# A decoder layer in float32: all gate and up weights prepared beside the attentions, three pairs of blocks by two levels, one look at the kept sums

## The chip, the cores and the metric

The kernel runs on one core of a Trainium2 chip. The metric is the device time of one execution in microseconds (us). The kernel before took 2239.64, 2241.54 and 2240.38 us in three runs; their median is 2240.38 us.

## The reference

x has 16 batches of 128 rows and 1024 columns, all in float32. Three sublayers follow one another, each on a layer norm (LN) and each added to x:

```python
x = x + attn(LN(x))           # one head of 256: softmax(q k^T / 16) v, then Wo
x = x + xattn(LN(x), ctx)     # "linear attention", 8 heads of 64
x = x + ffn(LN(x))            # h = silu(g) * u; h @ Wd^T
```

In the cross attention, queries come from LN(x) and keys and values from a second input. Queries pass through a softmax over the 64 entries of a head, keys through a softmax over the 1024 places of the sequence. A head's context is the product of its keys and values, queries are multiplied with it and projected, and each column of the result is divided by its length.

In the feed-forward part g and u are products of 1024 with 2752 columns (gate and up) and the way back is one of 2752 with 1024 (down). The weights are given as 4-bit numbers, two to an integer. Each group of 64 along a row has a scale and a zero point, and a weight is (number - zero) * scale.

## The kernel before, in words

**Strassen.** The feed-forward products use Strassen's scheme: a product of 2x2 blocks with seven multiplications in place of eight. The 2752 columns of gate and up form eleven blocks of 256 (`BLOCKS`, L42); the last, `RB` = 10, is smaller. `one_block` (L1178) uses one level: 14 products (seven of gate, seven of up), each of four matmuls with 512 columns. `two_levels` (L1360) takes a pair of blocks and uses Strassen twice: seven outer products, each with seven inner ones of four matmuls with 256 columns, 196 in all. Its operands are sums made in time: `ti` (right, by VectorE, `Operands.inner_right`, L1305) and `li` (left, by GpSimd, `inner_left`, L1338). In the trace a float32 matmul shows as two instructions.

**Passes.** The feed-forward part does eight batches (8 to 15) in pass 0 and the other eight in pass 1, and each pass goes over all blocks. `PAIRS` (L1068) lists the pairs that pass 0 does by two levels: only pair 3 (blocks 6 and 7). So its order is blocks 0 to 5, pair 3, blocks 8 and 9, and the last block (`last_block`, L1207). Pass 1 does all five pairs by two levels, then the last block. The down projection follows.

**Preparation of the weights.** `prepare` (L205) is a generator; each `next` is a step of work for VectorE. For each matrix of a block it takes two halves, loads them (`load_raw`, L172, on SyncE's queue, SP), splits the 4-bit numbers (two TENSOR_SCALARs into `pa`) and applies zero point and scale (two TENSOR_TENSORs). A third step makes four sums (`comb`, into `pc`). The seven Strassen combinations are stored to device memory (`wprep`). Gate and up of blocks 0 to 4 (`EARLY` = 5, L286) are prepared within the self attention, with stores on GpSimd's queue (L309). All the rest (gate and up of blocks 5 to 10, and down of all blocks, alternating) is prepared beside the blocks of pass 0, step by step from `beside` (L1567) and from the `between` of `two_levels`. `attention_done` (L1036) starts that.

**The cross attention.** The batch loop (L941 to L966) handles batch k and prepares batch k+1. Each batch has eight ticks: four `key_unit`s (L711) of the next batch and four `query_unit`s (L784) of its own, alternating. What comes later hangs in a list by hand: `later(n, fn)` (L616) runs fn n ticks on. A key unit makes keys (`kq`), their exponentials (`ek`, ScalarE, L727), their sum over the batch (`ksum`, VectorE) and the product with the second input (`kx`). After the fourth, `mix` (L755, two ticks later) forms the context and multiplies it into one matrix `m_sb`. A query unit makes queries and their exponentials (`qe`, ScalarE, L795). One tick later `weigh` (L802) sums each head's exponentials (`qden`), takes the reciprocal (`qrec`) and lets GpSimd multiply (`qe` times `qrec`, L806). Another tick later `turn` (L811) transposes the result on VectorE (`kt`). It is stored and read back in another order as `qs` by SP's queue. `project_out` (L848) multiplies `qs` with `m_sb`. The norms follow (L871 to L878: a square, then Ln and Exp on ScalarE). At the start, loads stand on SP in this order: the cross attention's four weight matrices and two small ones (L641 to L646), the second input for two batches (`cx` and `cxt`, L925), and `wo_again`, the output weights of the self attention, whose last batches are projected here (L926 to L937). `mix_weights` (L674) multiplies value and output weights per head. It runs before the first batch.

**Checks on the sums.** The kernel guards against overflow. `note` (L656) adds every batch's sums of exponentials and their reciprocals into two running totals on GpSimd. `raise_flag` (L662) compares the totals with a limit and counts the partitions that are within it, by one small matmul. If not all are, `kernel` (L1831) runs a slower form of the layer. `preload_act_table_set` (L672) loads one table of functions for ScalarE that holds both Ln and Exp.

**Weight loads.** `load_weights` (L1077) loads the prepared tiles in the order `to_load`, `AHEAD` = 4 of them (L1056) before the first block: the first on GpSimd's queue, the others on SP (L1561). The rows of x for pass 1 are loaded by `block_loads` (L551), one step after every third product of blocks 8 and 9.

Of the kernel before, what the change touches and what calls it, by code (L numbers as in the profile page):

```python
# [18 lines left out]
P = 128  # L19
# [47 lines left out]
def decoder_layer(  # L67
# [95 lines left out]
    def prep_pools(stack, name, c, ahead):  # L163
        for key, bufs in (("a", 3), ("c", c), ("raw", ahead + 1), ("sz", ahead + 1)):
            pools[key] = stack.enter_context(
                tc.tile_pool(name=f"{name}_{key}", bufs=bufs, side="right", reuse_waits="tile")
            )
# [4 lines left out]
    def load_raw(blk, mat, s):  # L172
# [3 lines left out]
        if mat == "d":  # L176
            raw, sz = raw[:w], pools["sz"].tile([P, 2, 512], F32, name="szd")[:w]
            nc.sync.dma_start(raw, dq[ds(start // 2, w), ts(s, 512)])
            for g in range(w // 32):
                row = dsz[start // GROUP + g, ts(s, 1024)].rearrange("(t f) -> t f", t=2)  # L180
                nc.sync.dma_start(sz[ts(g, 32)], row.partition_broadcast(32))
# [13 lines left out]
        for m, off, w in parts:  # L195
            q, szs = matrices[m]
            nc.sync.dma_start(raw[:, :, ds(at, w)], q[:, :, ds(off, w)])
            nc.sync.dma_start(
# [6 lines left out]
    def prepare(jobs, ahead, queue, vector=nc.vector):  # L205
# [3 lines left out]
        loads = deque(load_raw(*u) for u in units[:ahead])  # L209
# [6 lines left out]
        for k, (blk, mat, s) in enumerate(units):  # L216
# [6 lines left out]
            if k + ahead < len(units):  # L223
                loads.append(load_raw(*units[k + ahead]))
# [61 lines left out]
    EARLY = 5  # L286

    def give_half(b, h, oT, wo_d, psum, tensor=nc.tensor, vector=nc.vector):
# [19 lines left out]
    prep_pools(first, "q", 4, 1)  # L308
    early = prepare(  # L309
        [(blk, mat) for blk in range(EARLY) for mat in "gu"], 1, nc.gpsimd, InOrder(tc, nc.vector)  # L310
    )
    give_pool = ExitStack()
    ag = give_pool.enter_context(tc.tile_pool(name="a_g", bufs=1, reuse_waits="tile"))
    with (
# [166 lines left out]
        for t in range(NT):  # L481
# [38 lines left out]
            else:  # L520

                for i in range(1, BPT):
                    give((t - 1) * BPT + i - 1, oT)
                    value(i, xnT, v)
                atT = turn_weights(at)
# [76 lines left out]
    bcx = unit_pool("b_cx", 2)  # L602
    bw = unit_pool("b_w", 1)
    b0 = unit_pool("b_0", 2)
    bek = unit_pool("b_ek", 3)
    bas = unit_pool("b_as", 1)
    b3 = unit_pool("b_3", 3)
    bkt = side_pool("b_kt", 3)
# [3 lines left out]
    bqs = side_pool("b_qs", 5)  # L612
    b1 = side_pool("b_1", 1)
    b2 = side_pool("b_2", 2)
    bps = side_pool("b_ps", 3, space=PSUM)

# [15 lines left out]
    if True:  # L632
        wq_sb = bw.tile([P, HIDDEN], F32, name="wq_sb")
# [7 lines left out]
        sync.dma_start(wk_sb, xwk)  # L641
        sync.dma_start(wq_sb, xwq)
        sync.dma_start(wv_sb, xwv.rearrange("(r p) s -> p r s", p=P))
        sync.dma_start(xwo_sb, xwo.rearrange("(r p) o -> p r o", p=P))
        sync.dma_start(xbo_sb, xbo)
        sync.dma_start(gs_sb, xg)  # L646
        vector.tensor_scalar(gs_sb, gs_sb, math.sqrt(S), None, ALU.mult)
        vector.memset(ones, 1.0)
        if plain:

            totals = [bs.tile([P, 2 * HEADS], F32, name=f"total{n}") for n in range(2)]
            for t in totals:
                nc.gpsimd.memset(t, 0.0)

        def note(*both):
            if plain:  # L656
                for t, v in zip(totals, both):
                    t = t[:, : v.shape[1]]
                    nc.gpsimd.tensor_tensor(t, t, v, ALU.add)

        def raise_flag():

            within = [small.tile([P, 1], F32, name=f"within{n}") for n in range(2)]
            for w, t in zip(within, totals):
                vector.tensor_reduce(w, t, AX.X, ALU.add)
                vector.tensor_scalar(w, w, LIMIT, None, ALU.is_le)
            vector.tensor_tensor(within[0], within[0], within[1], ALU.mult)
            ps = bps.tile([P, 1], F32, name="mm")
            tensor.matmul(ps, ones, within[0], start=True, stop=True)
            vector.tensor_copy(flag, ps[0:1])  # L670

        tc.keep_in_program_order(nc.scalar.preload_act_table_set("natural_log_exp_and_others"))  # L672
# [16 lines left out]

        def load_ctx(b):  # L690
            c = bcx.tile([P, C], F32, name="cx")
            sync.dma_start(c, cx[b])
            ct = bct.tile([P, NB, S], F32, name="cxt")
            sync.dma_start(ct, cxt[b])
            return c, ct
# [15 lines left out]
        def key_unit(ctx, p, st):  # L711
# [17 lines left out]
            def use():  # L729
# [16 lines left out]
                if p == 3:  # L746
# [4 lines left out]
                    later(2, lambda: mix(st))  # L751
# [3 lines left out]
        def mix(st):  # L755
# [7 lines left out]
            ksum, krec = (small.tile([P, 4], F32, name=name) for name in ("ksum", "krec"))  # L763
            vector.tensor_copy(ksum, ks)
            vector.reciprocal(krec, ksum)
            note(ksum, krec)
# [17 lines left out]
        def query_unit(xn, pair, qs, wait):  # L784
# [3 lines left out]
            for i in range(2):  # L788
                tensor.matmul(
                    ps[:, i, :], xn[:, ts(2 * pair + i, P)], wq_sb, start=True, stop=True  # L790
# [11 lines left out]
            def weigh():  # L802
                den, rec = (small.tile([P, 2 * HEADS], F32, name=n) for n in ("qden", "qrec"))
# [3 lines left out]
                note(den, rec)  # L807
# [114 lines left out]


        batches = [p + i for p in PASSES for i in range(HB)]
        ctxs = {b: load_ctx(b) for b in batches[:2]}  # L925
        wo_again = []  # L926
        for d in range(2):
            wo_again.append(bqs.tile([P, C], F32, name="wo_again", tag="qs"))
            sync.dma_start(wo_again[d], wo[ts(d, P)])
        mix_weights()  # L930
# [7 lines left out]
        keys = {b: {} for b in batches}  # L938
# [3 lines left out]
        for k, b in enumerate(batches):  # L942
# [13 lines left out]
            if len(ahead) == 2:  # L956
                later(2, lambda n=ahead[1]: ctxs.update({n: load_ctx(n)}))
# [3 lines left out]
            for oc in range(4):  # L961
# [3 lines left out]
                query_unit(xns[b], oc, qs, 4 if len(ahead) == 2 else 3)  # L965
# [60 lines left out]
    with ExitStack() as gs:  # L1026
# [9 lines left out]
        def attention_done():  # L1036

            nonlocal rest
            if plain:
                raise_flag()  # L1040
            sides.close()
            prep_pools(second, "f", 4, 2)
            jobs = []
            down = deque((blk, "d") for blk in range(len(BLOCKS)))
# [856 lines left out]
```

## Time and profile before

| | |
|---|---|
| median of three runs | 2240.38 us |
| the profiled execution | 2241.3 us |
| its span in the trace | 2239.5 us |
| instructions | 24114 |
| DMA | 425.23 MB, mean 190 GB/s |
| self attention | 0 to 250 us |
| cross attention | 250 to 757 us, a batch every 31.2 us |
| gate and up, pass 0 | 757 to 1297.5 us |
| of it pair 3 by two levels | 1074.6 to 1163.6 us |
| gate and up, pass 1 | 1297.5 to 1760 us |
| down projection | 1760 to 2239.5 us |

All times are from the profile of one execution. Its engines are TensorE (PE: matmuls; PEld: its weight loads), VectorE (DVE), ScalarE (ACT), GpSimd (POOL) and SyncE (SP, which issues DMAs). A row of the windows gives a stretch of time, its length, and the busy time and number of instructions of PE, PEld, DVE, ACT and POOL. After these come the granted clock of PE, the share of time in which the DMA engines were busy, and GB/s. A row of the waits gives engine, tile and line of the waiting instruction, what it waited for, the total in us, the number of waits and the longest. A row of the timeline gives start, duration, engine, line, operation, and output from input; a wait stands in brackets. L63 is the line of a helper (`InOrder`, L55) that keeps instructions in the order of the program, so one goes by the names of the tiles.

### The profile page before, as it was taken

Reading aid. Unit: us, or ns where it says so; the run is one execution under the profiler, and the core shown is the slowest. Engines: PE = TensorE matmul, PEld = TensorE weight load, DVE = VectorE, ACT = ScalarE, POOL = GpSimd, SP = SyncE. Lnnn points to the kernel's source line nnn. Section 1 sums busy time; section 2 is a strip of 40 time slices with the busy share of each in tenths; the row PEclk is TensorE's granted clock in tenths of the full one; section 3 lists DMA queues with packets and bytes.
Section 4 is the critical chain, followed back from the end, with each engine's and each line's share of the span. In section 5 each row is a group of like instructions: output and inputs, shape, how many; then the busy total and the mean of one; then the engine's idle time right before and its main releaser. Section 6 shows DMA issues by size and latency. Waiting matters only on the chain.

```text
span 2239.5 us, 24114 instructions
## 1 busy us (share of the span) xinstructions
PE 2204.4 (98%) x8330; PEld 1517.3 (68%) x8330; DVE 1482.2 (66%) x2055; ACT 468.9 (21%) x651; POOL 553.1 (25%) x543
## 2 busy tenths in 40 slices
PE   8999899999999999999999999999999999999998
PEld 7556555555555544444774488888887688888887
DVE  6997466667667657666796658787787645544462
ACT  2111135454554431111111112121121000000000
POOL 5452044444444400001320044444442000000000
PEclk9999999999999999999999999999999999999999
DMA  6435246666686768887649834454554964333731
GB/s 251 157 130 169 85 132 198 209 205 197 208 258 192 225 182 287 284 267 253 199 166 301 251 100 158 167 197 155 175 198 165 350 211 164 114 125 129 226 118 39
DMA packets 270835, 425.23 MB, mean 190 GB/s; under 512 B 28784, under 2 KB 130544, under 8 KB 270576
## 3 DMA queue, kind: packets, MB, share of 16 engines
q1 hardware_dynamic: 244624, 377.72, 52.5%
q0 software_dynamic: 8064, 27.27, 3.3%
q10 hardware_dynamic: 18016, 18.62, 2.7%
q8 instruction: 68, 1.11, 0.2%
q14 instruction: 63, 0.52, 0.1%
HBM read 265.62 MB, written 157.35 MB: 189 GB/s over the span
## 4 chain that ended last, share of the span: by engine, by line
PE 90%; DVE 6%; issue 2%; DMA 1%; POOL 1%; ACT 0%; SPq 0%; DVEq 0%; POOLq 0%; ACTq 0%
PE po L1780 21%; PE q L63 20%; PE p L63 18%; PE kq L63 9%; PE mm L63 8%; PE kx L63 5%; PE mm L396 4%; PE mm L411 2%; DVE pa L63 2%; PE p L1157 1%; PE mm L292 1%; PE tr L343 1%; DVE ti L63 1%; DMA wo_again<-in_wo 0%; POOL qe L806 0%
## 5 line engine op out<-in xcount | busy, mean ns | idle before, releaser
L63 PE MATMUL p<-b,w 128*128 128x512 f32 x560 | 248.2, 596 | 1.9 <-DVE sg L63 1.9
L63 PE MATMUL q<-ti,li 128*128 128x256 f32 x1008 | 232.2, 379 | 3.5 <-DVE ti L63 2.8
L63 POOL TENSOR_TENSOR li<-w 128x512 f32<-128x512 f32 x84 | 118.1, 1408 | 433.3 <-DMA w<-wu 244.8
L63 PEld LDWEIGHTS q<-ti,li 128*128 128x128 f32 x1008 | 191.0, 190 | 31.3 <-issue 2.8
L63 PEld LDWEIGHTS p<-b,w 128*128 128x128 f32 x560 | 106.9, 191 | 136.4 <-issue 128.8
L1780 PE MATMUL po<-wc,lc 128*128 128x256 f32 x840 | 183.4, 379 | 0.0
L63 PE MATMUL p<-T,w 128*128 128x512 f32 x400 | 177.2, 592 | 0.0
L1780 PEld LDWEIGHTS po<-wc,lc 128*128 128x128 f32 x840 | 159.6, 190 | 21.8
L63 ACT COPY k<-q 128x512 f32<-128x512 f32 x126 | 73.7, 585 | 399.2 <-PE q L63 399.2
L63 PEld LDWEIGHTS p<-T,w 128*128 128x128 f32 x400 | 76.0, 190 | 95.7 <-issue 95.2
L1780 PE MATMUL po<-wq,lq 128*128 128x256 f32 x560 | 126.7, 379 | 0.2 <-issue 0.2
L806 POOL TENSOR_TENSOR qe<-qe,qrec 128x1024 f32<-128x1024 f32 x64 | 122.0, 1906 | 11.5 <-DVE qrec L63 9.3
L63 PEld LDWEIGHTS mm<-qs,m_sb 128*128 128x128 f32 x512 | 97.3, 190 | 40.1 <-issue 26.8
L63 PE MATMUL kq<-wk_sb,cx 128*128 128x512 f32 x256 | 120.4, 592 | 2.5 <-DMA cx<-in_cx 2.5
L63 PE MATMUL kx<-ek,cxt 128*128 128x512 f32 x256 | 121.8, 598 | 0.0
L63 PE MATMUL mm<-qs,m_sb 128*128 128x256 f32 x512 | 120.8, 379 | 0.0
L63 PE MATMUL kq<-wq_sb,xn 128*128 128x512 f32 x256 | 120.3, 593 | 0.0
L1780 PEld LDWEIGHTS po<-wq,lq 128*128 128x128 f32 x560 | 106.0, 190 | 15.8 <-issue 0.8
L63 DVE TENSOR_TENSOR pa<-pa,sz 128x1024 f32<-128x1024 int32 x86 | 112.6, 1309 | 2.5
L396 PE MATMUL mm<-xnT,wqkv_sb 128*128 128x512 f32 (+1 forms) x320 | 112.9, 509 | 0.0
L63 DVE STREAM_TRANSPOSE kt<-qe 128x1024 f32<-128x1024 f32 x64 | 79.5, 1242 | 43.7 <-POOL qe L806 43.5
L727 ACT ACTIVATE ek<-kq 128x1024 f32<-128x1024 f32 x64 | 65.3, 1020 | 147.4 <-PE kq L63 147.4
(201 smaller groups left out, 3595.7 us busy)
## 6 DMA issues: line engine op xcount, KB each, us to landing
w<-wu SPq DMA_DIRECT2D x140, 256.0 KB, 3.6
lq<-h SPq DMA_DIRECT2D x140, 256.0 KB, 4.4
w<-wg SPq DMA_DIRECT2D x138, 256.0 KB, 2.8
kd<-kt SPq DMA_DIRECT2D x64, 512.0 KB, 2.9
qs<-kd SPq DMA_DIRECT2D x256, 128.0 KB, 3.2
h<-hc SPq DMA_DIRECT2D x80, 256.0 KB, 2.8
wq<-wd SPq DMA_DIRECT2D x70, 256.0 KB, 5.3
h<-h SPq DMA_DIRECT2D x60, 256.0 KB, 3.0
```

The costliest lines, as they stand in the source:

```text
L63: return lambda *args, **kw: self._tc.keep_in_program_order(fn(*args, **kw))
L292: tensor.matmul(ps, oT[:, d, ts(b % BPT, S)], wo_d[d][:, ts(h, 512)], start=(d == 0), stop=(d == 1),)
L343: nc.tensor.transpose(tr[:, j, :], xn[:, ts(4 * h + j, P)], ident)
L396: nc.tensor.matmul(ps[:, tokens], wqkv_sb[:, f, c, :], xnT[:, c, tokens], start=(c == 0), stop=(c == CC - 1),)
L411: nc.tensor.matmul(ps, xnT[:, c, ts(i, S)], wqkv_sb[:, 4:6, c, :], start=(c == 0), stop=(c == CC - 1),)
L727: nc.scalar.activation(ek, ps, AF.Exp)
L806: nc.gpsimd.tensor_tensor(qe, qe, rec.unsqueeze(2).to_broadcast(wide), ALU.mult)
L1157: tensor.matmul(ps, wt[:, j, :], T[q][:, :, j], start=(first == q and j == 0), stop=(q in (2, 3, 4) and j == JC - 1), skip_group_check=True,)
L1780: nc.tensor.matmul(bank[:, i, :], l[:, ts(i, S)], w,  start=(start and c == 0 and i % 2 == 0), stop=(stop and c == len(pairs) - 1), skip_g ...
```

## The change

1. A list `todo` holds all jobs of preparation: gate and up of blocks 0 to 9, the last block's two, then all of down. The self attention takes 11 of them (before: 10), with three more steps at its end. A second generator, `middle`, takes the other 11 of gate and up and runs within the cross attention. Batches 0, 2, 4, 6 and 8 take three steps, the other batches up to 12 take two. Its loads and stores stand on SP in the order of the program. Only down is left for the blocks.
2. `PAIRS` is [2, 3, 4]: pass 0 does blocks 0 to 3 by one level, blocks 4 to 9 by two, then the last block. The steps of preparation per pair fall from three to two, and those beside the blocks move.
3. The sums of exponentials are kept, each in its own columns of one tile `sums` (128 x 1088). `raise_flag` looks at their largest and smallest once, after the attention; the counting matmul comes two ticks later. `note` and the additions on POOL are gone.
4. `preload_act_table_set` is gone. The built program has 36 table loads where there were 9.
5. The first loads of the cross attention have a new order (`wk`, `cx` and `cxt` of the first batch, `wo_again`, then the others). `mix_weights` runs four ticks later, and `mix` four ticks after the last key unit, not two.
6. All four of the first weight tiles are loaded on GpSimd's queue. The rows of x for pass 1 are loaded at once after the pairs.
7. Pools: preparation has three or two `pa` buffers in place of three, `kt` two in place of three, `qs` four in place of five, and the pools are opened in another order.

```diff
@@ prepare, early preparation
+    todo = [(blk, mat) for blk in range(RB) for mat in "gu"] + [(RB, "r"), (RB, "m")]
+    todo += [(blk, "d") for blk in range(len(BLOCKS))]
+    EARLY, MIDDLE = 11, 22
...
-    prep_pools(first, "q", 4, 1)
-    early = prepare(
-        [(blk, mat) for blk in range(EARLY) for mat in "gu"], 1, nc.gpsimd, InOrder(tc, nc.vector)
-    )
+    prep_pools(first, "q", 3, 1)
+    early = prepare(todo[:EARLY], 1, nc.gpsimd, InOrder(tc, nc.vector))
...
                     value(i, xnT, v)
+                    next(early, None)
@@ cross attention: pools
-    bkt = side_pool("b_kt", 3)
+    bkt = side_pool("b_kt", 2)
...
-    bqs = side_pool("b_qs", 5)
+    bqs = side_pool("b_qs", 4)
...
+    prep_pools(sides, "x", 2, 1)
+    middle = prepare(todo[EARLY:MIDDLE], 1, sync, vector, sync)
@@ cross attention: first loads, sums, flag
-        sync.dma_start(wk_sb, xwk)
-        sync.dma_start(wq_sb, xwq)
...
+        nc.sync.dma_start(wk_sb, xwk)
+        ctxs = {batches[0]: load_ctx(batches[0])}
+        wo_again = []
+        for d in range(2):
+            wo_again.append(bqs.tile([P, C], F32, name="wo_again", tag="qs"))
+            nc.sync.dma_start(wo_again[d], wo[ts(d, P)])
+        nc.sync.dma_start(wq_sb, xwq)
...
-        def note(*both):
-            if plain:
-                for t, v in zip(totals, both):
-                    t = t[:, : v.shape[1]]
-                    nc.gpsimd.tensor_tensor(t, t, v, ALU.add)
+            sums = bs.tile([P, B * 4 * 2 * HEADS + B * 4], F32, name="sums")
...
-            for w, t in zip(within, totals):
-                vector.tensor_reduce(w, t, AX.X, ALU.add)
-                vector.tensor_scalar(w, w, LIMIT, None, ALU.is_le)
+            for w, op, limit, test in zip(
+                within, (ALU.max, ALU.min), (LIMIT, 1 / LIMIT), (ALU.is_le, ALU.is_ge)
+            ):
+                vector.tensor_reduce(w, sums, AX.X, op)
+                vector.tensor_scalar(w, w, limit, None, test)
...
-        tc.keep_in_program_order(nc.scalar.preload_act_table_set("natural_log_exp_and_others"))
+            later(2, count)
@@ key_unit, weigh, batch loop
-                    later(2, lambda: mix(st))
+                    later(4, lambda: mix(st))
...
-                note(den, rec)
...
-        mix_weights()
+        later(4, mix_weights)
...
+            for n in (3, 5, 7) if k in (0, 2, 4, 6, 8) else (3, 7) if k < 13 else ():
+                later(n, lambda: next(middle, None))
@@ attention_done
-            for blk in range(EARLY, len(BLOCKS)):
-                jobs += [(blk, mat) for mat in ("gu" if blk < RB else "rm")]
-                jobs.append(down.popleft())
-            jobs += down
-            rest = prepare(jobs, 2, nc.sync, vector)
+            rest = prepare(todo[MIDDLE:], 2, nc.sync, vector)
@@ gate and up, pass 0
-        PAIRS = [3]
+        PAIRS = [2, 3, 4]
...
-            load_weights(nc.gpsimd if n == 0 else nc.sync)
+            load_weights(nc.gpsimd)
...
                 elif blk == RB:
-                    steps = n in (0, 2, 4)
+                    steps = n in (0, 1, 2)
                 else:
-                    steps = (1, 1 + (mat == "g" and blk < 3), 1, 0, 1, 0, 0)[n % 7]
+                    steps = (1, 1, 1, 0, 1, 0, 0)[n % 7]
...
-            if pass1 and n % 3 == 0:
-                next(pass1_loads, None)
...
-                    0, PAIRS, first_operands, lambda q: q in (1, 6, 5) and next(rest, None)
+                    0, PAIRS, first_operands, lambda q: q in (1, 6) and next(rest, None)
...
-                pass1_loads = block_loads(1, pass1)
+                for _ in block_loads(1, pass1):
+                    pass
```

## The prediction

> **What bounds the kernel now.** I read the page's busy times first, then the windows by stage, the chain of waits, the waits of TensorE (PE), and last the timeline of one batch of the cross attention.
>
> ```profile
> PE 2204.4 (98%) x8330; PEld 1517.3 (68%) x8330; DVE 1482.2 (66%) x2055; ACT 468.9 (21%) x651; POOL 553.1 (25%) x543
> ```
>
> PE is busy for 2204.4 of 2239.5 us, so there are two ways to a shorter time: less matmul work, or some of the 35 us in which PE stands. Next the windows (PE busy, weight loads, DVE, ACT, POOL, granted clock, DMA share): one batch of the cross attention, a later batch with the heaviest DMA, and the one pair done by two levels in pass 0.
>
> ```profile
> 502.50:533.70 31.20, 31.20 (x112) 17.78 (x108) 21.79 (x28) 15.93 (x19) 13.69 (x16) 1.00 0.66 203
> ...
> 658.70:690.00 31.30, 31.30 (x111) 17.85 (x109) 21.79 (x28) 15.90 (x19) 13.68 (x16) 1.00 0.85 272
> ...
> 1074.60:1163.60 89.00, 85.67 (x394) 74.14 (x393) 75.27 (x91) 15.74 (x25) 35.18 (x24) 1.00 0.50 163
> ```
>
> In the attention PE has no gap at all, and VectorE (DVE) is busy 21.8 us of a batch's 31.2: 9.4 us are free. A DMA share of 0.85 costs PE nothing there. In the pair PE stands 3.3 us. The chain gives the price of a matmul where PE runs without a break (start, duration, number of instructions):
>
> ```profile
> 249.84 9.81 DMA wo_again<-in_wo
> ...
> 1163.59 133.90 PE p L63 x312
> ...
> 1378.35 343.87 PE q L63 x1592
> ```
>
> A matmul of 512 columns takes 133.90 / 312 = 0.4292 us, one of 256 takes 343.87 / 1592 = 0.2160 us (the program's one matmul is two of these instructions). PE's own waits name nearly all of its idle time outside the start and the tail:
>
> ```profile
> PE p L1157 <- DMA w<-wg: 4.9, 1, 4.9
> PE q L63 <- DVE ti L63: 3.3, 4, 2.4
> PE mm L63 <- DMA wo_again<-in_wo: 3.1, 1, 3.1
> PE kq L63 <- DMA cx<-in_cx: 2.5, 1, 2.5
> ```
>
> **1. Blocks 4, 5, 8 and 9 by two levels: -23.0 us.** I counted the instructions of the two built programs by shape. The changed one has 224 fewer matmuls of 512 columns and 392 more of 256: two pairs, each 112 replaced by 196. 448 x 0.4292 = 192.3 us go, 784 x 0.2160 = 169.3 us come. Nothing stands beside this: PE is the path.
>
> **2. Stalls in the two new pairs: +5 us.** The pair in the trace loses 3.3 us because `ti` (the right operands of the inner level, DVE) is late: 0.2 + 0.4 + 0.3 us beside preparation steps, and 2.4 us at 1154.7, at the last outer product, where DVE has eleven additions of q = 7, two products for h and four operands, some of them held up by POOL's `li`. The changed pairs have two preparation steps instead of three. So 2.5 us for each new pair; bounds 0 (pass 1's five pairs run without a break, but they keep most operands) and 2 x 4.3.
>
> **3. Start of the cross attention: -4 us.** PE stands 2.5 us for `cx` and 3.1 us for `wo_again`, because six and ten transfers are queued ahead of them on SP, all from 244.7 on. In the new order `cx` is second and `wo_again` third and fifth. `cx` needed 6 us from issue to landing; issued at 245.2 it is there at about 251, when PE has finished at 250.4. The products of mix_weights, which ran in that gap, move to the fourth tick. Bounds -5.6 (both waits gone) and 0.
>
> **4. End of the attention and the flag: -1.5 us.** The first weights are issued by POOL at 759.70 behind a product of `qe`; in the new order they stand one product earlier. But the weight loads of that matmul also waited for ACT's last `qe`, which waited for the transpose `kt` (759.61), which waited for POOL. That chain loses only m_sb's 0.7 us and its wait, so I take 1 us of the 4.9. The flag's matmul no longer makes PE wait (0.6). The two reductions over all 1088 kept sums, two of 128x1024 at 1.2 us instead of 0.15, lie in DVE's gaps of block 0. Bounds -5.5 and +3 (two of the new table loads fall on this chain, see 5).
>
> **5. Preparation inside the cross attention: +9 us.** This is the doubtful term. Eleven jobs (31 steps) that ran beside blocks 0 to 9 move there. A step on one half of a matrix is two TENSOR_SCALARs of 0.42 and two TENSOR_TENSORs of 1.22 us, 3.2 us from start to start; a step of four sums (0.68) is 2.5; a job 8.9. Batches 0, 2, 4, 6, 8 get three steps (8.9 us), the others up to 12 two (5.9). By busy time it fits: 21.8 + 8.9 = 30.7, and 27.7. But DVE does not use all its time, and these rows show why (start, duration, wait):
>
> ```profile
> 514.91 1.16 DVE L63 TENSOR_TENSOR ksum<-ksum,ek 128x1024 f32<-128x1024 f32 x1
> ...
> 516.10 1.90 POOL L806 TENSOR_TENSOR qe<-qe,qrec 128x1024 f32<-128x1024 f32 x1
> ...
> 518.03 1.25 DVE L63 STREAM_TRANSPOSE kt<-qe 128x1024 f32<-128x1024 f32 x1 [1.96 <-POOL qe L806]
> ...
> 520.81 1.90 POOL L806 TENSOR_TENSOR qe<-qe,qrec 128x1024 f32<-128x1024 f32 x1
> ...
> 521.69 2.10 DVE L63 TENSOR_TENSOR ksum<-ksum,ek 128x1024 f32<-128x1024 f32 x1
> ```
>
> DVE and POOL exclude each other: POOL's product starts only when ksum is done, and the next ksum lasts 2.10 instead of 1.16 us, to 1.1 us after POOL's end. The preparation's operations do the same: at 86.9 a `pa` beside POOL's addition took 2.8 instead of 1.2 us. I walk through one batch of the new DVE order. Its own instructions without such holds take 20.3 us. After the second reciprocal ksum goes first, POOL's 1.9 us follow, and the preparation behind it waits: 1.9. The third: 1.0, as above. The fourth: `y` goes first, POOL's product follows, and `kt` needs it: 2.0. Small ones 0.4. Together 5.3 us, so a three-step batch takes 20.3 + 8.9 + 5.3 = 34.5 and a two-step batch 31.5, against PE's 31.2. Batches 2, 4, 6, 8 each put DVE 3.3 us behind, seven others 0.3: 15.3 us. What hides part: ACT may write the third next `qe` only after `kt` has read the buffer, and that had 9.4 us to spare (535.6 + 1.25 to 546.2, one batch of 31.2 added to the row at 504.4); one preparation step of 3.2 us now stands ahead of it, so 6 are left. 15.3 - 6 = 9. Behind a late DVE stand the row shifts, for which ACT waits in order, and behind ACT the PSUM tiles of keys and queries, of which there are two.
>
> ACT itself gets dearer. Without the preload the build puts 36 table loads in place of 9, two around each batch's Ln. The rows of ACT in one batch:
>
> ```profile
> 528.65 1.02 ACT L727 ACTIVATE ek<-kq 128x1024 f32<-128x1024 f32 x1 [1.13 <-PE kq L63]
> ...
> 529.57 0.59 ACT L877 ACTIVATE sq<-mm 128x512 f32<-128x512 f32 x1
> ...
> 530.99 1.06 ACT L878 ACTIVATE sq<-sq 128x1024 f32<-128x1024 f32 x1
> ...
> 532.08 1.02 ACT L795 ACTIVATE qe<-kq 128x1024 f32<-128x1024 f32 x1
> ```
>
> With 1.28 us twice (a load at 786.04, the next operation at 787.33), `qe` ends at 529.67 + 1.28 + 1.2 + 1.28 + 1.06 + 1.02 = 535.5 instead of 533.1. PE wants that PSUM tile for the next but one product at 535.3, now that the mix (1.9 us) has left this place: 0.3 us lost in each of 14 batches, 4 us, unless DVE is the later one anyway; so it is inside the 9. The Trainium skill, ScalarE: Activation LUTs, section What ACT_TABLE_LOAD costs, speaks against the change: it adds a drain of about 1.4 us to each load. By that rule, as an estimate, `qe` would end 2.8 us later still and the 4 us would be some 43; the row, where the next operation starts 1.29 us after the load, shows no drain, and it decides. Bounds of the whole term: 0 and +25.
>
> **6. The rest: 0.** The job added to the self attention (8.9 us of DVE) falls into 191 to 250, where DVE is busy 41.4 of 59 us; bound +2. The pass-1 loads of x come together after the pairs: eight of 512 KB, 6 us to landing each, needed some 17 to 21 us into the last block (its first two products take 13.9 us), whose own weights are already queued ahead of them; bound +6. The adds of `total` on POOL go with nothing behind them. SP's queue carries the moved loads and stores between `kd` and `qs`; `qs` had 9 us to spare and the DMA rows above show room.
>
> **Sum:** -23.0 + 5 - 4 - 1.5 + 9 = -14.5. The profiled execution took 2241.3 us (span 2239.5); 2241.3 - 14.5 = 2226.8. It lay 0.9 above the median of the runs, so 2226.
>
> **Rivals.** (a) The cover holds: DVE finds the moved work room because the holds overlap with waits I counted twice; term 5 is 0 to 4, the time 2217 to 2221. For it: 9.4 us free per batch. Against it: the holds above. (b) DVE becomes the bound: every preparation step meets one POOL product and loses 1.9 us, as `pa` did beside POOL's additions. A three-step batch then takes 34.5 + 2 x 1.9 = 38.3, a two-step batch 33.4; batches 2 to 12 lose 4 x 7.1 + 7 x 2.2 - 6 = 38 us instead of 9, and the time is 2255, slower. It turns slower when a batch of the first thirteen takes on average over 33.0 us: the other terms bring 23.5 us (23.0 - 5 + 4 + 1.5), and 23.5 / 13 = 1.8 above 31.2 eats them. (c) The two levels do not give what the count says: a stall of 11.5 us in each pair would eat the gain; the one pair in the trace had 3.3. Then 2244.
>
> **Chances.** Forecast (2222 to 2233) 0.42; (a) 0.33; on the way to (b) or (c), 2233 to 2245, 0.17; (b) beyond 2245, 0.08. The range takes the bounds of term 5, 0 and 25 with the small ones: 2212 to 2241. About 0.2%, 4.5 us, is what runs of this kernel can tell from no change: faster (below 2235.9) 0.42 + 0.33 + 0.06 = 0.81, same 0.11, slower 0.08.
>
> **What would show it.** 448 fewer and 784 more PE instructions of the two shapes, 0.2160 us each; `ti` as a wait of PE of some 8 us in all; the wait for `wo_again` gone; batches 2 to 9 longer than 31.2 us with DVE over 29 us busy and PE waiting for ACT, ACT for DVE; 36 table loads. Wrong, if batches stay at 31.2 (then a), or if DVE falls behind by more than POOL's products explain.

## The result, and the profile after

In seven runs each the changed kernel took 2250.83 us (2247.06 to 2256.00), the kernel before 2241.33 us (2238.72 to 2243.49). The ratio is 1.0045, 95% interval 1.0033 to 1.0057: **slower by 9.5 us**, where 14 us less were forecast; the forecast's widest bound was 2241. The profiled execution is the longest of the seven, 2256.0 us with a span of 2254.2; it is compared with the 2239.5 us of before, and why the seven differ is taken up below.

The busy times of the changed kernel (share of the span, instructions):

```profile
PE 2201.5 (98%) x8666; PEld 1588.1 (70%) x8666; DVE 1611.7 (71%) x2185; ACT 512.0 (23%) x690; POOL 594.9 (26%) x450
```

PE has 336 instructions more (784 - 448), as counted. But its busy time fell by 2.9 us, not by 23, and its idle time rose from 35.1 (2239.5 - 2204.4) to 52.7 us. Where it stands now, from the waits of PE (total, times, longest):

```profile
PE mm L63 <- DMA qs<-kd: 10.9, 4, 6.3
PE q L63 <- DVE ti L63: 10.6, 8, 3.3
...
PE mm L63 <- DMA wo_again<-in_wo: 4.9, 2, 3.4
PE mm L63 <- DVE within L63: 2.9, 1, 2.9
PE kq L63 <- ACT qe L807: 1.6, 1, 1.6
PE mm L63 <- DVE ksum L63: 1.6, 2, 1.1
```

The first row is new: it is the cross attention. The second was 3.3 and is now 10.6: it is the pairs. Marks on PE's timeline give the time by stage:

| stretch, us | before | after | difference |
|---|---|---|---|
| start to first product of block 0 | 762.7 | 785.4 | +22.7 |
| from there to the start of pass 1 | 534.6 | 525.9 | -8.7 |
| pass 1 to the down projection | 462.5 | 462.5 | 0.0 |
| down projection to the end of the span | 479.7 | 480.4 | +0.7 |

In the cross attention the distances from mix to mix, from the second on, were 31.23 us each. Now the quiet ones are 31.48, and the others 32.0 to 40.9. The windows of one batch and of the first pair (PE busy, weight loads, DVE, ACT, POOL, clock, DMA share):

```profile
380.00:412.00 32.00, 32.00 (x110) 17.89 (x109) 29.33 (x37) 18.91 (x22) 11.27 (x7) 1.00 0.87 273
...
999.43:1090.80 91.37, 87.35 (x390) 75.79 (x389) 72.11 (x87) 15.87 (x25) 38.78 (x27) 0.96 0.44 139
```

DVE was busy 21.8 us of a batch and is now busy 29.3 of 32. In the pair, PE works at a mean clock of 0.96. What that is shows the timeline of PE (start, duration, instructions, wait) at the pair's longest gap, and the windows around it (clock third from the end):

```profile
1074.65 1.89 PE L63 MATMUL q<-ti,li 128*128 128x256 f32 x8
1079.83 3.75 PE L63 MATMUL q<-ti,li 128*128 128x256 f32 x8 [3.29 <-DVE ti L63]
1083.37 3.13 PE L63 MATMUL q<-T,w 128*128 128x256 f32 x8
1086.34 1.89 PE L63 MATMUL q<-ti,li 128*128 128x256 f32 x8
```

```profile
1076.00:1078.00 2.00, 0.54 (x3) 0.14 (x1) 2.00 (x2) 0.59 (x1) 2.00 (x2) 1.00 0.00 0
...
1080.00:1082.00 2.00, 2.00 (x5) 1.64 (x6) 1.48 (x3) 1.02 (x1) 0.00 (x0) 0.50 0.00 0
1082.00:1084.00 2.00, 2.00 (x6) 1.55 (x6) 1.29 (x2) 0.36 (x2) 0.27 (x1) 0.50 0.19 74
```

After the 3.3 us of waiting, eight instructions take 3.75 us instead of 1.89: for 6.8 us, from 0.8 us before the wait ends, PE has half its clock. **So this wait costs its own length and 3.0 us more.** Before the tail of the program, the profile of before has three such stretches with 13.7 us in all, that of after nine with 44.4 us. Of these, 1.3 and 4.1 us lie within waits; half of the rest is lost work, 6.2 and 20.1 us. The difference, 13.9 us, is most of the 20 us of busy time that did not go away.

So the difference of the two spans, 14.7 us, is made of 23.0 us of matmuls less, 17.6 of idle time more, 13.9 more lost to the clock, and 6.2 left over. Of these, 3.75 are the 0.25 us that each of 15 batches is longer, with PE shown as busy.

### The profile page after: what moved, and what is told of

The parts are those of the page before. It is cut to its first block, busy times and chain, and to the rows that moved or that the text cites. A ratio compares the mean times of both kernels' runs of the same rounds, so it can differ in the third digit from the quotient of the medians.

```text
span 2254.2 us, 24858 instructions
## 1 busy us (share of the span) xinstructions
PE 2201.5 (98%) x8666; PEld 1588.1 (70%) x8666; DVE 1611.7 (71%) x2185; ACT 512.0 (23%) x690; POOL 594.9 (26%) x450
## 4 chain that ended last, share of the span: by engine, by line
PE 76%; DVE 14%; DMA 3%; issue 3%; POOL 2%; ACT 1%; SPq 0%; DVEq 0%; POOLq 0%; ACTq 0%
PE q L63 26%; PE po L1783 21%; PE p L63 10%; PE kq L63 4%; PE mm L63 4%; PE mm L397 4%; DVE pa L63 3%; PE kx L63 2%; PE mm L412 2%; DVE kt L63 2%; PE p L1160 2%; DVE sums L63 1%; PE mm L295 1%; DVE ti L63 1%; DVE pc L63 1%
## 5 line engine op out<-in xcount | busy, mean ns | idle before, releaser
L63 PE MATMUL q<-ti,li 128*128 128x256 f32 x1344 | 315.4, 384 | 11.0 <-DVE ti L63 10.2
L63 PEld LDWEIGHTS q<-ti,li 128*128 128x128 f32 x1344 | 257.6, 192 | 49.8 <-issue 9.9
L63 POOL TENSOR_TENSOR li<-w 128x512 f32<-128x512 f32 x112 | 159.9, 1429 | 258.2 <-DMA raw<-in_dq 140.6
L63 ACT COPY k<-q 128x512 f32<-128x512 f32 x168 | 98.4, 585 | 540.1 <-PE q L63 540.1
L819 POOL TENSOR_TENSOR qe<-qe,qrec 128x1024 f32<-128x1024 f32 x64 | 145.3, 2270 | 249.8 <-DVE qrec L63 206.3
L1783 PEld LDWEIGHTS po<-wc,lc 128*128 128x128 f32 x840 | 159.6, 190 | 21.8
L63 PE MATMUL mm<-qs,m_sb 128*128 128x256 f32 x512 | 124.9, 388 | 10.9 <-DMA qs<-kd 10.9
L63 PE MATMUL p<-b,w 128*128 128x512 f32 x304 | 133.9, 592 | 0.0
L63 POOL TENSOR_TENSOR li<-w,li 128x512 f32<-128x512 f32 x56 | 75.5, 1347 | 209.3 <-PE q L63 207.1
L63 PE MATMUL q<-b,w 128*128 128x256 f32 x512 | 120.9, 379 | 0.0
L63 DVE TENSOR_TENSOR C<-q,k 128x512 f32<-128x512 f32 x120 | 82.2, 685 | 53.4 <-PE q L63 51.2
L63 PEld LDWEIGHTS p<-b,w 128*128 128x128 f32 x304 | 57.8, 190 | 71.9 <-issue 69.8
```

Source lines behind the costliest of these rows:

```text
L63: return lambda *args, **kw: self._tc.keep_in_program_order(fn(*args, **kw))
L819: nc.gpsimd.tensor_tensor(qe, qe, rec.unsqueeze(2).to_broadcast(wide), ALU.mult)
L1783: nc.tensor.matmul(bank[:, i, :], l[:, ts(i, S)], w,  start=(start and c == 0 and i % 2 == 0), stop=(stop and c == len(pairs) - 1), skip_g ...
```

## The experiments

Each is a variant of the changed kernel. "First product" is the start of block 0 on PE, "pass 0" the time from there to pass 1; both are from the profiled execution. The ratio is to the kernel before, run beside each variant.

| run | first product | pass 0 | median us | ratio to before |
|---|---|---|---|---|
| before | 762.7 | 534.6 | 2241.33 | |
| after | 785.4 | 525.9 | 2250.83 | 1.0045 [1.0033, 1.0057] |
| e1 table loaded once | 777.3 | 524.3 | 2248.40 | 1.0031 [1.0020, 1.0043] |
| e2 transfers only | 767.9 | 518.1 | 2238.72 | 0.9992 [0.9982, 1.0001] |
| e3 arithmetic only | 774.1 | 523.3 | 2243.05 | 1.0006 [0.9996, 1.0016] |
| e4 GpSimd's queue | 782.4 | 521.3 | 2251.32 | 1.0049 [1.0032, 1.0066] |
| e5 `ti` of q = 4 loaded | 781.0 | 508.8 | 2236.13 | 0.9980 [0.9971, 0.9990] |
| e6 fewer steps in the attention | 760.0 | 552.9 | 2256.90 | 1.0071 [1.0056, 1.0087] |
| e7 start and flag | 778.0 | 518.0 | 2249.81 | 1.0042 [1.0027, 1.0057] |
| e8 e5, e6 and e7 | 758.0 | 540.6 | 2242.91 | 1.0009 [1.0000, 1.0018] |
| e9 two steps per batch | 757.4 | 519.3 | 2222.00 | 0.9914 [0.9901, 0.9928] |
| e10 three and two steps | 773.9 | 513.6 | 2232.53 | 0.9965 [0.9952, 0.9978] |
| e11 tail of the attention | 754.6 | 511.7 | 2208.87 | 0.9858 [0.9842, 0.9874] |
| e12 e11 with one pair | 753.9 | 528.1 | 2227.32 | 0.9940 [0.9924, 0.9957] |

### e1: the table of Ln and Exp loaded once

```diff
+        tc.keep_in_program_order(nc.scalar.preload_act_table_set("natural_log_exp_and_others"))
```

> The changed kernel with the one line back that loads the table holding both Ln and Exp at the start of the cross attention (9 table loads instead of 36). In the trace of the changed kernel a batch of the cross attention takes 31.48 us at best, against 31.23 before, and 15 distances between batches add up to 25.9 us more than before. Theory ACT (the table loads delay the exponentials): the undisturbed batch returns to 31.23 us, and the long batches of 33 to 41 us too, because a late qe is behind them: 2225 to 2230 us. Theory DVE (VectorE has too much to do) and theory QUEUE (the preparation's loads and stores stand between kd and qs on SP): only the 0.25 us per batch come back, some 4 us, and the waits of PE for qs (10.9 us) stay: 2246 to 2248 us.

2248.4 us, 2.4 less than the changed kernel. The quiet batches are back at 31.23 us, and the last is 1.9 us shorter. The first product comes 8 us earlier, but the waits for `qs` stay (10.6 us). The table loads cost 0.25 us per batch, about what was forecast, and are not the cause of the long batches.

### e2 and e3: the transfers without the arithmetic, and the arithmetic without the transfers

```diff
+            if not bare:                      # e2: stored is the raw tile
                 vector.tensor_tensor(pair, pair.bitcast(I32), zero, ALU.subtract)
                 vector.tensor_tensor(pair, pair, scale, ALU.mult)
...
+            if bare:                          # e3: nothing is stored
+                stores.clear()
```

> The changed kernel in which the 31 steps of preparation within the cross attention issue all their loads and stores but make no arithmetic: what is stored is the raw tile, so the weights of blocks 5 to 10 are wrong, and VectorE has 8.9 or 5.9 us less to do per batch. Theory DVE: the waits for qs and ksum and the long batches go, only the 0.25 us per batch from the table loads stay: the cross attention is some 22 us shorter than in the changed kernel, 2228 to 2232 us. Theory QUEUE (or the load on the DMA engines): the waits for qs stay, and the time is above 2242 us.

> The counterpart: the 31 steps within the cross attention do all their arithmetic on VectorE, but load only once and store nothing (the blocks 5 to 10 then read the prepared weights of blocks 0 to 4, so these blocks are wrong and the later loads the same). Theory DVE: the long batches stay, 2247 to 2253 us. Theory QUEUE: the waits for qs go, 2228 to 2234 us. If both this and the run without arithmetic are fast, the two needed each other: a late kt on VectorE and a busy queue.

Neither theory alone holds. Without the arithmetic, one long batch stays (36.8 us) and the waits for `qs` fall to 4.0 us; without the transfers, many batches of 32 to 34 us stay and the waits for `qs` fall to 3.8. First mix to last mix took 458.1 us before, 467.4 with transfers only, 473.4 with arithmetic only, 484.0 with both. Less 3.75 us for the table loads, that is +5.6, +11.5 and +22.2, so both together cost 5 us more than the sum of the two. But that is the clock: the stretches at half clock lose 0, 1.7 and 8.1 us in this part of the three profiles. Without them it is 5.6, 9.8 and 14.1: each costs time by itself, and nothing shows that the two need each other. DVE's waits between 290 and 700 us say how; of before, of the changed kernel, and of the one with transfers only:

```profile
DVE ksum L63 <- PE mm L63: 70.8, 12, 6.8
DVE kt L63 <- POOL qe L806: 30.2, 16, 2.0
```

```profile
DVE kt L63 <- POOL qe L819: 21.7, 12, 2.1
DVE kt L63 <- DMA kd<-kt: 9.7, 3, 5.9
...
DVE ksum L63 <- PE mm L63: 0.3, 1, 0.3
```

```profile
DVE kt L63 <- DMA kd<-kt: 56.9, 15, 7.3
```

Before, DVE was early and waited 70.8 us for PE. In the changed kernel it waits 0.3 us for PE: it is the late one. With transfers only, it waits 56.9 us for the store of `kt` (two buffers instead of three). PE bears most of that, since DVE has time again.

e2 shows the other effect too. Its profiled execution took 2229.8 us at a mean clock of 0.997, the ten others 2237.3 to 2242.7 at 0.992 to 0.994: the same program, with more or fewer of its waits followed by half clock.

### e4: the preparation's transfers on GpSimd's queue

```diff
-    middle = prepare(todo[EARLY:MIDDLE], 1, sync, vector, sync)
+    middle = prepare(todo[EARLY:MIDDLE], 1, InOrder(tc, nc.gpsimd), vector, InOrder(tc, nc.gpsimd))
```

> The changed kernel with the loads and stores of the preparation within the cross attention on GpSimd's queue, not between kd and qs on SP. The transfers and VectorE's work are the same. Theory QUEUE: PE's waits for qs (10.9 us and the slow clock after them) go: about 2235 us. Theory DVE: the waits stay; and GpSimd, which now waits in order for the tiles to be stored, delays its products of qe: 2250 us or more.

2251.3 us, and PE still waits 11.4 us for `qs`. So the place on SP's queue alone is not it: ahead of the longest wait in this run the store of `kt` itself takes 12.1 us from issue (651.44) to landing. What is left is `kt`, which is late, and its way to device memory: in the changed kernel the store takes 4.1 us (median between 290 and 700 us) at a DMA share of 0.81, before 2.9 us at 0.67. That these two make up all of it is argued, not shown.

### e5: the operands of the last outer product loaded

```diff
+            def save(self):
+                for step in self.inner_right(4):
+                    step()
+                self.saved = dram.tile([P, 4, HT // Q, CHUNKS, Q], F32, name="ti4", tag="ti4")
+                sync.dma_start(self.saved, self.R[4])
...
+            def load(self):
+                R[4] = self.pool.tile([P, 4, HT // Q, CHUNKS, Q], F32, name="ti", tag="ti", bufs=2)
+                nc.sync.dma_start(R[4], self.saved)
```

> The changed kernel, but the right inner operands of outer product q = 4 (the ti that PE waits for 3.3, 3.3 and 2.2 us near the end of each pair of pass 0) are made once, beside block 3, kept in device memory and loaded again in every pair, so that VectorE has four operations less in the outer product before. Theory WORK (in the outer product q = 7 VectorE has 17 operations of 0.69 us and GpSimd four of 1.28 us, and those on SBUF alone exclude each other: 16.9 us against PE's 12.35): the three waits go, with the stretches of slow clock after them; a pair takes 86 to 87 us instead of 91.4, and the time is 2236 to 2240 us against 2250.8 of the changed kernel. Rival: the wait only moves to the next product or to the load (256 KB times four per pair on SP): a pair stays above 90 us and the time above 2246 us.

As the theory had it: 2236.1 us, and the three waits are gone. The first pair (its window):

```profile
995.00:1080.70 85.70, 84.96 (x394) 74.50 (x393) 69.39 (x86) 15.78 (x25) 38.59 (x27) 1.00 0.54 177
```

85.7 us instead of 91.4, at full clock. So the wait came from the work of DVE and GpSimd in the outer product before (q = 7), which has no step of preparation: with four of DVE's operations less it is gone.

### e6, e7 and e8: fewer steps in the attention, a later start and flag, and all together

```diff
-    EARLY, MIDDLE = 11, 22
+    EARLY, MIDDLE = 11, 18                                       # e6, with e1's line
-    bkt = side_pool("b_kt", 2)
+    bkt = side_pool("b_kt", 3)
+            for n in () if k > 13 else (5,) if k % 2 else (3, 7):
-                    steps = (1, 1, 1, 0, 1, 0, 0)[n % 7]
+                    steps = (1, 1, 1, 1, 1, 0, 1)[n % 7]
...
-                n + 1,                                            # e7: give_half
+                n + 3,
-            later(2, count)
+            later(5, count)
```

> The changed kernel with three things in the cross attention: the table of Ln and Exp loaded once, three buffers for kt instead of two, and only 7 of the 11 jobs (21 steps, two and one per batch in turn over 14 batches); the last four jobs stand beside blocks 1 to 3, which get 12 steps each instead of 8. By the runs so far the arithmetic alone and the transfers alone each lengthen the cross attention (first mix to last mix) to 473.4 and 467.4 us of which 3.75 us are table loads, both together to 484.0; before it was 458.1. Theory DVE AND QUEUE together: with 21 steps both have room again and a batch is 31.23 us; 458 to 462 us, and the time is 2225 to 2230 us. Rival (blocks 1 to 3 cannot take the steps: VectorE late there, PE waits for sg): the gain of 24 us is partly given back, 2235 to 2240 us.

> The changed kernel with the six projections of wo_again two ticks later (two more products of keys and one of values stand before them) and the flag's counting matmul three ticks later. Theory: both waits for wo_again (5.0 us with 3.4 us lost to the slow clock after them) and the one for the flag's two reductions (2.9 us with 1.7) are waits for something that comes a little later in any case, so other products fill them: 2239 to 2243 us against 2250.8. Rival: a wait of the same length appears elsewhere (cxt for the first product of values, the first weights at the end), 2247 us or more.

> All three sets of edits together. If they add up: 2251 - 12 - 23 - 9 = 2207 us; if the slow clock depends only on the sum of PE's idle time, somewhat less. Theory CLOCK (every idle stretch of PE of about 1 us or more can bring 3.4 or 6.8 us at half clock after it, so a wait costs up to twice its length): granted clock above 0.996 with fewer such stretches, and fewer differences between runs. Rival (the stretches of slow clock come at any case in such a dense program): the clock stays at 0.992 and 2217 us or more.

**e6** took 2256.9 us, more than either theory said. The cross attention did as expected (first to last mix 459.6 us), but pass 0 takes 27 us more. PE's waits:

```profile
PE p L63 <- DVE h L63: 15.3, 2, 10.3
PE mm L63 <- DVE within L63: 10.6, 1, 10.6
```

The first row comes from the four jobs beside blocks 1 to 3. The second, 7.7 us longer than in the changed kernel, is the tail of the attention in block 0, the subject of e11. With 12 steps per block DVE runs out of `pa` buffers: from 830 to 1004 us it waits 21.8 us for stores of `pa`, in the changed kernel 6.6 us. e8 has the same blocks; in its timeline of DVE a step waits for the store of an earlier one, and behind it and the next step stands the read-out `h`, for which PE waits 12.2 us (until 997.4):

```profile
979.63 0.76 DVE L63 TENSOR_SCALAR pa<-raw 128x512 int32<-128x512 int32 x2 [4.05 <-DMA wd<-pa]
...
992.38 4.37 DVE L63 TENSOR_TENSOR pa<-pa,szd 128x1024 f32<-128x1024 int32 x2
...
996.68 0.68 DVE L63 TENSOR_TENSOR h<-p,k 128x512 f32<-128x512 f32 x1
```

**e7** took 2249.8 us, not 2239 to 2243. Its later projections brought the first product 7.4 us forward, though PE now waits 3.2 us for `cxt` there, as the rival said. Where the flag made PE wait, it now waits 3.5 us for `h`. And a wait of 4.6 us for `li` at the start of pass 1, followed by 6.8 us at half clock, is in no other run; why is open. **e8** has quiet batches but for one (36.9 us). In pass 0 (540.6 us) it pays 16.6 us of waits beside the jobs, as e6 does, and 11.2 us at the tail of the attention: 2242.9 us, not 2207, at a clock of 0.991.

### e9 and e10: two steps per batch, against three and two

```diff
+    EARLY, MIDDLE = 11, 20                                        # e9 alone
+            for n in (3, 7) if k < 14 else ():                    # e9 alone
+                    steps = n in (0, 1, 2, 4)                     # e9 alone, last block
+                    0, PAIRS, first_operands, lambda q: q in (1, 6, 5) and next(rest, None)  # e9 alone
...
+                    later(7 + 3 * n, lambda: next(loads))         # both
+                later(1 + n, lambda each=each: look(*each))       # both: the flag's two reductions
```

Both also have e1's line, e5, three buffers of `kt` and the later projections of e7.

> The changed kernel with the edits that the runs so far speak for: ti of q = 4 loaded (as in e5), wo_again's projections two ticks later (as in e7), the table of Ln and Exp loaded once and three buffers for kt (as in e6); and, new, exactly two steps of preparation in each of the first 14 batches of the cross attention (9 jobs, 27 steps; the last block's two jobs go beside the pairs, three steps each again), the loads of x for the first block a tick further apart, and the flag's two reductions in ticks of their own. Unlike e6, blocks 1 to 3 keep 8 steps each. Theory STEPS (a batch has room for two steps, not for three: batches with two took 31.23 us in e6 wherever nothing else was late): the cross attention from first to last mix takes 458 to 463 us instead of 484, blocks 0 to 3 214, the three pairs 258 instead of 274: 2208 to 2216 us. Rival QUEUE (the transfers of the preparation are as dense in 14 batches as in 13): one or two batches above 35 us around 640 to 690 stay, 2217 to 2225 us.

> The same as the run before it, but with the changed kernel's own distribution of the 31 steps in the cross attention (three in batches 0, 2, 4, 6, 8, two in the others up to 12), and its steps in the pairs: what tells the density of the steps from the table load, the buffers of kt and the loads of x. Theory STEPS: batches above 32 us remain behind those with three steps; the cross attention from first to last mix is 12 to 20 us longer than with two steps each, and the time 2222 to 2235 us. Rival (kt's two buffers and the loads of x made the long batches, not the number of steps): the same time as with two steps each, within 4 us.

STEPS holds for the cross attention: first to last mix takes 461.2 us with two steps and 479.3 with three and two, 18.1 more, and the times differ by 10.5 us. PE's waits for `qs`, of e9 and of e10:

```profile
PE mm L63 <- DMA qs<-kd: 2.8, 1, 2.8
```

```profile
PE mm L63 <- DMA qs<-kd: 11.1, 6, 4.8
```

e9 has 27 of the 31 steps and the same load on the DMA engines (share 0.83 against 0.81 between 290 and 700 us), so the number of steps in a batch decides, not the load on the DMA engines. One batch of 34.3 us is left in e9, where the loads of x for block 0 run. There SP's queue is on the path: between a store of `kt` (issued at 661.80) and the next read of `qs` (668.50) SP issues stores and loads of the preparation (662.22 to 667.9). e9's 2222.0 us lies in the rival's range, not in 2208 to 2216; what keeps it from there are PE's waits of 3.5 us for the first weights and 8.2 us within block 0, which are next.

### e11: the tail of the attention

DVE's timeline of e9 in block 0:

```profile
820.98 1.23 DVE L63 SCALAR_TENSOR_TENSOR y<-sq,y 128x1024 f32<-128x1024 f32 x1 [23.52 <-ACT sq L895]
...
826.04 0.69 DVE L63 TENSOR_TENSOR h<-p,k 128x512 f32<-128x512 f32 x1
```

DVE has nothing to do for 23.5 us and still makes PE wait: `y` waits for ScalarE, and the read-out of PE's banks (`h`) stands behind `y` and 3.8 us of further steps for the last batch.

```diff
-                when = (10, 10, 11, 11, 12, 1, 0)
+                when = (10, 10, 11, 11, 12, 4, 0)
+            if plain and not ahead:
+                later(8, raise_flag)
-            load_weights(nc.gpsimd)
+            load_weights(nc.scalar if n == 0 else nc.gpsimd)
-                    steps = n in (0, 1, 2, 4)
+                    steps = n in (0, 1, 2, 4, 6)
```

> The kernel with two steps per batch (e9), whose PE still waits 8.3 us, and has 10.2 us at half clock after it, within block 0, and 3.5 us with 6.8 us at half clock for the first weights. Changes: the last batch's y (and what follows it on VectorE) three ticks later, so that products of block 0 read out by VectorE stand ahead of it; the flag's reductions right after the last sums, not after all else; the first weight tile loaded on ScalarE's queue; one step more beside the last block. Theory TAIL (VectorE, in order, waits at y for ScalarE's Exp of the last norms, and the bank of PSUM that PE needs is read out behind it): the wait falls to 0 to 3 us and the slow clock with it: 2222 - 8 to 13 for the wait, - 3 to 6 for the weights: 2204 to 2211 us. Rival (the read-out is late because of all the rest of VectorE's tail, not because of its place behind y): the wait stays at 5 us or more, 2216 us or more.

2208.9 us, 1.4% below the kernel before (0.9842 to 0.9874). The wait of 8.2 us for `h` and the one for the first weights are gone; one of 2.9 us for `sg` is left in block 0. The edit moves `y` and all that follows it behind the read-outs, so it does not tell the place behind `y` from the work after `y`. One batch of 36.2 us is still left in the cross attention. The busy times:

```profile
PE 2180.5 (99%) x8666; PEld 1582.7 (72%) x8666; DVE 1612.1 (73%) x2177; ACT 478.4 (22%) x663; POOL 597.7 (27%) x448
```

This is the changed kernel's number of matmuls with 21 us less busy time, 15.3 of them by the clock: 10.2 us at half clock are left, where there were 44.4.

### e12: what the second level is worth

```diff
-        PAIRS = [2, 3, 4]
+        PAIRS = [3]
```

> The fastest version so far (e11, 2208.9 us) with only pair 3 by two levels, as in the kernel before: what the second level itself is worth once its stalls are gone. By the count (448 x 0.4292 - 784 x 0.2160 us) the four blocks take 23.0 us more by one level; in e11 the three pairs take 86.27 us each, where two blocks take 96.14 us, so 2 x 9.87 = 19.7 us more. Theory COUNT: 2228 to 2232 us. Rival (the second level gives back part of the gain in VectorE's work beside it, so that one level frees the rest of pass 0): 2220 us or less.

2227.3 us, 18.5 more than e11 and just under the range of COUNT; the rival is out. The second level of two pairs saves 18.5 of the 23 us in the medians (15.8 between the two profiles), if its operands come in time.

## Why the prediction was wrong, step by step

- **Term 1, the matmuls, -23.0:** right. The instructions are as counted, and e12 finds 18.5 us in the median with the remaining small stalls in it.
- **Term 2, stalls in the pairs, +5:** mis-sized. The three pairs take 274.1 us where their matmuls take 254.0 (3 x 392 x 0.2160), 20.1 lost; the one pair of before lost 4.3. So +15.8: 7.3 us of waits more, and 7.7 us lost to half clock, which the step put at nothing. The waits themselves came near the forecast (10.6 us, where it said some 8) and at the place it named, the last outer product; e5 shows that the work of the outer product q = 7 is enough for them.
- **Term 3, the start, -4:** it failed. `wo_again` is issued at 250.34, not earlier: SP waits 5.2 us there for PE's last product of the self attention (the row below this list). The wait for `cx` is gone, as forecast, but PE waits 4.9 us for `wo_again`, with 6.8 us at half clock, against 3.4 before. e7 takes this wait away; 3.2 us of waiting for `cxt` come instead.
- **Term 4, the end, -1.5:** better than forecast for the first weights: the wait for them (4.9 us, with 6.8 us of half clock) became 0.4 of waiting for `qe`. They were issued 6.4 us before the first product (779.03 and 785.41), before only 3.0 (759.70 and 762.71); how much of that is the attention's own lateness is not shown. The flag's wait, which was to go, grew from 0.6 to 2.9 us.
- **Term 5, the preparation, +9:** this step failed. Mix to mix, 15 distances are 25.9 us longer. That DVE falls behind was right, and so were the 0.25 us per batch for the tables. The path from DVE to PE was not: by the prediction it ran over the row shifts and ACT to the PSUM tiles, and PE would wait for ACT, while `qs` had 9 us to spare and stood at nothing. Between the first and the last mix PE waits 10.9 us for `qs`, 1.6 for `ksum` and 1.9 for ACT; 8.1 us are lost to half clock, and the remaining 3.5 go to the tables. So the late DVE reaches PE by `kt`, its store and the read of `qs`, and every part of this way got longer: POOL's product ahead of `kt` takes 2.27 us instead of 1.91 (means), the store 4.1 instead of 2.9, the read 3.3 instead of 3.1 (medians), and `kt` has a buffer less (e2 loses 5.6 us without any arithmetic). The clock was not in the sum either: four of the six waits for `qs` and `ksum` brought it, and 17.1 of the 44.4 us at half clock are between 285 and 700. Rival (b) said that it turns slower above 33.0 us per batch in the first thirteen, and the thirteen distances from the second on have a mean of 33.1. That this agrees so closely is luck: the point supposes that the other terms bring 23.5 us, and they brought some 11 (25.9 - 14.7, from the two spans).
- **Term 6:** right within 1 us for pass 1 and the down projection; what it says of `qs` failed, as under term 5.

The wait of SP ahead of `wo_again` (term 3):

```profile
SPq L660 <- PE mm L467: 5.2, 1, 5.2
```

**The common error** is a price that stood in the profile of before, and that every term put at nothing: the clock. The prediction cited the granted clock of three windows, all 1.00. Two others of the same profile, with waits of PE in them (clock third from the end):

```profile
250.00:290.00 40.00, 34.29 (x91) 15.79 (x90) 13.61 (x28) 10.93 (x13) 2.73 (x4) 0.96 0.29 105
...
757.00:803.00 46.00, 41.11 (x116) 22.71 (x115) 24.40 (x30) 19.12 (x25) 15.04 (x18) 0.93 0.80 240
```

They hold stretches of 3.4 and 6.8 us at half clock, behind the waits for `wo_again` and for the first weights. By this, the forecast's waits of PE would have cost up to twice their length. It also explains much of the spread: the seven runs have mean clocks of 0.989 to 0.994, the runs of the kernel before, beside the variants, 0.995 to 0.997. At a span of 2250 us, 0.003 in the mean are 6.8 us, most of the 9.5 us between the medians (an estimate from these clocks). At full clock the two kernels would be about equal, as an estimate: 2239.5 - 6.2 = 2233.3 and 2254.2 - 20.1 = 2234.1 us. There the 23 us are eaten by 17.6 us of idle time and the 6.2 us left over, tables included.

## What to carry to other kernels

An engine that is 70% busy on average has no 30% to give away: count, per period of the loop, its work plus its waits for its partners, and keep room for the longest step, for here two steps per batch of 31.2 us were hidden in all batches but one, and three were not. Where TensorE is the bound, price each of its waits with the slow clock that follows, and look for that in the profile of before. An in-order engine that idles can still be the one that is late: look at what stands behind the instruction that waits.

## What the runs showed of the hardware

The half clock after waiting was the surprise. Count each slow stretch for the longest wait of PE near its start, in the 14 profiles up to 2150 us and without the very first wait of each: none of 114 waits of 0.3 to 1.1 us had one; of those of 1.1 to 2 us 7 in 32 had; of 2 to 3 us 21 in 33; of 3 to 3.4 us 13 in 18; of more, 20 in 21. The slow stretches last 3.4, 6.8, 10.2 or 13.7 us, multiples of 3.4. A stretch can begin within the wait, the longest by 5 us and more, so in no profile did one cost over 3.4 us of work. The same wait at the same place is followed by one in some runs and not in others (the 3.29 us before `ti` in e7 by none, in the changed kernel by 6.8 us). The Trainium skill, TensorE: Matmul & The Clock Gate, section What's actually happening, describes a gate with windows of 3413 ns that run freely, which fits both the multiples and the chance. Its section Why this matters for your kernels advises against gaps of more than about 3 us; the runs here show that gaps from 1.1 us on can bring the slow clock, and the measurement decides.
